# FFN weights turned by a transposing DMA on 16-bit planes instead of TensorE, with the background's turns redistributed

## The chip, the core and the metric

The kernel runs on one core of one Trainium2 chip, in one launch. The metric is device time in microseconds (us), the median of several executions. PE is TensorE, PEld its weight loads, DVE VectorE, ACT ScalarE, POOL GpSimd, and SP SyncE, which only issues DMAs here.

## The reference

One transformer block on x of shape (1, 2048, 1024), all in float32:

```python
x = x + attn(layernorm(x))        # q, k, v = xn @ w.T + b, seen as 32 heads of 32 channels
                                  # per token: softmax(q @ k.T / sqrt(32)) over the token's own 32 heads, then @ v
dq = lambda w: nf4_quant_dequant(w)   # per 64 values: absmax; nearest of 16 codes of w / absmax; code * absmax
h = silu(xn2 @ dq(w1).T) * (xn2 @ dq(w2).T)      # xn2 = layernorm(x); w1, w2: (2752, 1024)
x = x + h @ dq(w3).T                             # w3: (1024, 2752)
```

The scores are between the heads of one token, so they are many small 32 x 32 products. The quantising of w1, w2 and w3 is part of the computation and is done on the chip.

## The kernel before

**Three streams.** The foreground is first the attention, 16 tiles of 128 tokens, and then the FFN. In the background, from the first microseconds on, the FFN weights are quantised. A branch for inputs with other low bits (`fast=False`) is built too, and does not run here.

**Attention** (to about 569 us). For each tile i the loop from line 833 runs Q, K and V projections (`project`, L643: two halves of 16 matmuls each), the scores S and the weighted sums G (4 x 64 small matmuls in two parts), and `keep_T`, which transposes the normed tile and stores it to DRAM. Between them stand DVE's 32 x 32 transposes, its bias adds (L669, L685) and its softmax steps, and ACT's exponentials and norms.

**FFN.** There are 21 full chunks of 128 hidden rows, and one of 64. A `Unit` (L1406) does seven products of a Strassen-Winograd scheme for the gate and up projection of one chunk pair and 1024 tokens, eight matmul records each, into PSUM tiles z, q and rr. ACT copies z away between the products (L1424, L1431, L1438), and DVE multiplies gate and up (L1446, L1450). Behind the units of each of the first ten passes `down7` (L1509) does the down projection in seven products: ACT copies each result (L1532) and POOL issues accumulating DMAs into x1d in DRAM (L1534). There are 12 passes: six groups of chunks by two halves of the tokens; the last two end in the plain `down` (L1575). 41 units run after the plain first one; the page's L1446 x41 counts them.

**The background** is a Python generator, `background` (L283). It has 65 jobs: per chunk one for w1, one for w2 and one for w3, with a joint one for the half chunks of w1 and w2. Of these 63 have full blocks of 128 rows. A job takes a 128 x 1024 tile `wn` (3 buffers), scales it by its blocks' absolute maxima, makes eight band steps, and scales the result r (2 buffers) back. A band step is an ACT activation into an int8 tile (L299, 6 buffers) and a DVE add (L305; the first is L303). r goes to a second generator, `finish` (L205), which turns it in eight 128 x 128 blocks: four TensorE transposes into a PSUM tile `ptw` (L219), an ACT copy into the tile `wop` (L220), and both once more. When a pair is complete DVE makes the four sums and differences of the scheme (L226 to L229 and L232 to L235), and one DMA stores `wop` to DRAM (L238), from where `load_w12` (L455) and `load_w3` (L462) fetch it.

**What sets the order.** `advance(n)` (L357) adds n * 10/17 to an account, and takes one step of the generator for each whole turn. `spent(us)` does so in the FFN with us * RATE, after each product, and `flush` moves `finish` on. That gives an order in the program. The order on PE is the program's, since it is set by hand:

```python
    ctx.enter_context(tc.manual_schedule(engines={nc.tensor.engine}))
```

For ACT, DVE, POOL and SP a scheduler writes each engine's order at build time. It may draw an instruction forward past others when what it reads, and the buffer it writes, are free by its reckoning. On the chip each engine then works through its fixed order, and waits on semaphores. `hook["scale"]` tells who multiplies by the absolute maxima: ACT in the attention, DVE in `down7`, both in turn in the rest of the FFN.

Of the kernel before, what the change touches and what calls it, by code (L numbers as in the profile page):

```python
# [20 lines left out]
P = 128  # L21
# [11 lines left out]
HALF = F - NFULL * P  # L33
TB = 512
NTBP = S // (2 * TB)
RATE = 0.69
TURN = 10 / 17
XTAGS = ("B11", "B21", "B22", "T1", "T2", "T3", "T4")
XOPS = ("B11", "B12", "B21", "B22", "T1", "T2", "T3", "T4")
PAIRED = NFULL - 1  # L40
# [11 lines left out]
NNEG = 7  # L52
I8 = mybir.dt.int8
I32 = mybir.dt.int32
F32R = mybir.dt.float32r
LOW = 0xFFF

# [73 lines left out]
def forward(ctx, tc, const, fast, x, wqT, wkT, wvT, qb, kb, vb, w1, w2, w3, out):  # L131

    nc = tc.nc
    xf = x.flatten_outer_dims()
    of = out.flatten_outer_dims()
    ident, eps, mhalf = const["ident"], const["eps"], const["mhalf"]
# [15 lines left out]
    hook = {"scale": "ACT"}  # L152
# [49 lines left out]

    wops = {}

    def finish(kind, c, v):  # L205

        hn = min(P, F - c * P)
        q = hn if kind == "3" else P
        paired = kind == "3" and c < PAIRED
        second = kind == "2" or paired and c % 2  # L210
        if not second:
            wops["t"] = dqp.tile([P, 8, 4, P], FP, tag="wop", name="wop", bufs=1)
        o = wops["t"]
        first = 2 if second else 0
        for half in range(2):
            pt = hook["psum"](half)
            for k in range(4):
                j = 4 * half + k
                nc.tensor.transpose(pt[:q, k, :], v[:, j * q : (j + 1) * q], ident)  # L219
            nc.scalar.copy(o[:q, first + half], pt[:q])  # L220
            yield
        if kind == "1" or paired and not second:
            return
        if paired:
            b11, b12, b21, b22, t1, t2, t3, t4 = (o[:, n] for n in range(8))
            nc.vector.tensor_tensor(t1, b12, b11, ALU.subtract)  # L226
            nc.vector.tensor_tensor(t2, b22, t1, ALU.subtract)
            nc.vector.tensor_tensor(t3, b22, b12, ALU.subtract)
            nc.vector.tensor_tensor(t4, b21, t2, ALU.subtract)  # L229
        if kind == "2":  # L230
            a11, a12, a21, a22, s1, s2, s3, s4 = (o[:, n] for n in range(8))
            nc.vector.tensor_tensor(s1, a21, a22, ALU.add)  # L232
            nc.vector.tensor_tensor(s2, s1, a11, ALU.subtract)
            nc.vector.tensor_tensor(s3, a11, a21, ALU.subtract)
            nc.vector.tensor_tensor(s4, a12, s2, ALU.subtract)  # L235
        n = 8 if second else 2
        d = tc.dram_tile([q, n, 4, P], FP, name=f"wd{kind}_{c}")
        nc.sync.dma_start(d, o[:q, :n])  # L238
        wd[kind, c] = d
        if paired:  # L240
            wd[kind, c - 1] = d

    pending, step = [], {}
# [39 lines left out]
    def background():  # L283
        ready = load_w(*jobs[0])
        ahead = load_w(*jobs[1])
        am = absmax(*jobs[0], ready)
        yield
        for n, (kind, c) in enumerate(jobs):
            wn, wa = ready, am
            ready = ahead  # L290
            if n + 2 < len(jobs):
                ahead = load_w(*jobs[n + 2])
            w = width(kind, c)
            v = wn[:, :w]
            r = dqp.tile([P, E], FP, tag="r", name="r", bufs=2)[:, :w]
            for i, (lo, hi, scale, bias) in enumerate(BANDS):
                t = dqp.tile([P, E], I8, tag="sg", name="sg", bufs=6)[:, :w]
                with behind("step"):
                    nc.scalar.activation(t, v, AF.Copy, bias=bias, scale=scale)  # L299
                top = float(NF4_CODE[hi + 1])  # L300
                low = -1.0 if lo is None else float(NF4_CODE[lo])
                if i == 0:
                    nc.vector.tensor_scalar(r, t, top, low, ALU.min, ALU.max)  # L303
                else:
                    nc.vector._custom_dve(TENSOR_ADD_SAT, out=r, in0=r, in1=t, s0=top, s1=low)  # L305
                step["n"] = i
                yield
                if i == 4 and n + 1 < len(jobs):
                    am = absmax(*jobs[n + 1], ready)
                    yield  # L310
            engine = ("ACT", "DVE")[n % 2] if hook["scale"] == "both" else hook["scale"]
            scaled(r, r, wa, w // BLOCK, engine)
            pending.append(finish(kind, c, r))
            yield

    def low_bits():
# [40 lines left out]
    def advance(n):  # L357
        lent["turns"] += n * TURN
        while lent["turns"] >= 1:
            lent["turns"] -= 1  # L360
            with turn():
                next(bg, None)
# [99 lines left out]
    def load_w3(c):  # L462
# [10 lines left out]
            nc.sync.dma_start(t[r, :], src)  # L473
        return t

    def spent(us, finish=True):
        if finish and step["n"] in range(3, 8):
            flush(1)
        advance(us * RATE)

    def new_h():
        return hp.tile([P, TB], FP, tag="h", name="h", bufs=12)
# [48 lines left out]
    if fast:  # L531
# [111 lines left out]
        def project(m, i, n, take, first=lambda: None):  # L643

            ps = bank("pj")
            for k in range(KC):
                for part in xs[i]:
                    nc.tensor.matmul(  # L648
                        ps,
                        part[:, k, :],  # L650
                        W[m][k // 2][:, k % 2, ts(n, TB)],
                        start=k == 0 and part is xs[i][0],
                        stop=k == KC - 1 and part is xs[i][1],
                        skip_group_check=True,
                    )
            first()
            take(n, ps)
            advance(1)

        def qk(m, i, bias):  # L660
            tag = f"{m}d" if i != 1 else "xT1" if m == "q" else "xT0"
# [61 lines left out]
        def S(i, part):  # L723

            if not part:
                ats[i] = ps_at.tile([P, 4, 512], FP, tag="at", name="sc")
            at = ats[i]
            score(at, qd[i][0], kd[i][0], part)
            advance(1)
            if not part:  # L730
                return
            del qd[i], kd[i], ats[i]
            sc = at[:, :, 0:256].rearrange("p g (s t) -> p g s t", t=NH)
            mx = small.tile([P, 4, 8], FP, tag="mx", name="mx")
            nc.vector.tensor_reduce(mx, sc, AX.X, ALU.max)
            pr = work.tile([P, 32, NH], FP, tag="pr", name="pr")
            nc.vector.tensor_tensor(
                pr.rearrange("p (g s) t -> p g s t", g=4),
                sc,
                mx.unsqueeze(3).to_broadcast([P, 4, 8, NH]),  # L740
                ALU.subtract,
            )
            nc.scalar.activation(pr, pr, AF.Exp, scale=1.0 / math.sqrt(D))
            prT[i] = work.tile([P, 32, NH], FP, tag="prT", name="prT")
            nc.vector.transpose(prT[i], pr)

        def G(i, part):

            if not part:
                ats[i] = ps_at.tile([P, 4, 512], FP, tag="at", name="cx")  # L750
            at = ats[i]
            weigh(at, prT[i], part)
            advance(1)
            if not part:
                return
            del prT[i], ats[i]
            st = small.tile([P, 4], FP, tag="st1", name="st1", bufs=2)
            rs = small.tile([P, 4, 8], FP, tag="mx", name="rs")
            sums = at[:, :, : 8 * (D + 1)].rearrange("p b (s d) -> p b s d", d=D + 1)
            nc.vector.reciprocal(rs, sums[:, :, :, D])  # L760
            pr = work.tile([P, 32, NH], FP, tag="pr", name="pw")
            nc.vector.tensor_tensor(
                pr.rearrange("p (s b) d -> p b s d", b=4),
                sums[:, :, :, :D],
                rs.unsqueeze(3).to_broadcast([P, 4, 8, D]),
                ALU.mult,
            )
            x1 = xt.pop(i)
            cx = work.tile([P, E], FP, tag="cx", name="cx")
            nc.vector.transpose(  # L770
                cx.rearrange("p (h d) -> p d h", d=D), pr.rearrange("p s d -> p d s")
            )
            nc.vector.scalar_tensor_tensor(
                cx, x1, 1.0, cx, ALU.mult, ALU.add, accum_out=st[:, 0:1]
            )
            for n in range(2):
                nc.sync.dma_start(x1d[i][n], cx[:, ts(n, TB)])
            if i + 3 < NT:
                load_x(i + 3)
            hook["normed"] = norm(cx, cx, st, pr).ins  # L780
            x1n[i] = cx
# [51 lines left out]
        for i in range(2, NT):  # L833
# [28 lines left out]
            V(i, 1)  # L862
            flush(1)
            S(i, 0)
            advance(2)
        hook["scale"] = "both"
        left.close()

# [39 lines left out]
    else:  # L908
# [190 lines left out]
        with tc.issue_after(opening["first"]):  # L1099
            for n in range(2):  # L1100
                k = slice(2 * n, 2 * n + 2)
# [537 lines left out]
    for n, (g, tbp) in enumerate(passes):  # L1639
# [23 lines left out]
                hs[unit.c] = unit.last()  # L1663
        if sides:
            down7(g, tbp, sides)
        else:
            for _ in bg:
                pass
            down(g, tbp, hs)
# [41 lines left out]
```

## Time and profile before

| | |
|---|---|
| time, median of 3 runs (lowest, highest) | 2228.09 us (2227.78, 2230.97) |
| the profiled execution: its time, its span | 2224.73 us, 2222.9 us |
| busy of the span: PE, DVE, ACT, POOL | 96%, 63%, 59%, 12% |
| attention's tiles 2 to 16, from 67 to 569 us | DVE busy 417.28 us, PE 459.58 us, ACT 319.75 us |
| DMA, mean over the span | 181 GB/s |

The table's busy time is that of one profiled execution, from its first to its last instruction. A busy PE counts matmuls that overlap, so PE can read high where its matmuls are not dense. A group's row gives the line, engine, operation, tiles, and shapes; then the count, the busy time and the mean duration in ns, and last the idle time ahead of it with what ended it.

### The profile page before, as it was taken

To read this page: it belongs to the slowest core of one execution; us is meant where nothing else is said; L and a number is where in the kernel's file an instruction comes from. 1 tells how busy PE (TensorE), PEld (TensorE's weight loads), DVE (VectorE), ACT (ScalarE), POOL (GpSimd) and SP (SyncE) were. 2 spreads that over 40 slices of the span, in tenths; PEclk is the share of its full clock that TensorE was granted. 3 is DMA by queue.
4 is the path that set the end of the run, shared out by engine and by line. 5 is a ranking of instruction groups with operands and counts; after the bars stand their busy time and mean duration, and the time that the engine had idled before them with its cause. 6 is when DMAs were issued, how large, how long until landed. Compare 5 with 4: busy or idle time off the path is not lost.

```text
span 2222.9 us, 35192 instructions
## 1 busy us (share of the span) xinstructions
PE 2144.0 (96%) x14193; PEld 1148.3 (52%) x14193; DVE 1395.8 (63%) x1599; ACT 1302.8 (59%) x2635; POOL 275.4 (12%) x335
## 2 busy tenths in 40 slices
PE   7899989898999999999999999999999999999998
PEld 6677777776544444444444444444444444444432
DVE  6788877978666567565665756756656656453022
ACT  7667665756656657657657676586575676411200
POOL 1000000000003104013021030030120310401300
PEclk8899999999999999999999999999999999999999
DMA  8132323324669539579377694494983866965972
GB/s 294 40 126 68 116 68 107 119 85 160 239 240 263 140 123 250 191 266 196 125 196 190 247 243 133 148 224 165 320 181 123 182 173 256 259 208 141 259 286 96
DMA packets 154684, 402.73 MB, mean 181 GB/s; under 512 B 13648, under 2 KB 67920, under 8 KB 137360
## 3 DMA queue, kind: packets, MB, share of 16 engines
q1 hardware_dynamic: 113808, 326.92, 40.9%
q0 software_dynamic: 40704, 73.47, 19.6%
q8 instruction: 113, 1.85, 0.3%
q14 instruction: 59, 0.48, 0.1%
HBM read 227.07 MB, written 173.28 MB: 180 GB/s over the span
## 4 chain that ended last, share of the span: by engine, by line
PE 44%; issue 21%; DMA 5%; POOL 2%; DVE 1%; ACT 1%; POOLq 0%; SPq 0%; DVEq 0%; ACTq 0%
PE z L391 17%; PE q L391 8%; PE z L1519 7%; DMA x1d<-acc 4%; PE rr L391 4%; PE y L1519 4%; POOL x1d L1534 2%; PE r L1519 2%; PE po L1602 1%; PE ptw L219 1%; PE po L1613 1%; DMA wn<-in_wqT_dram 0%; DVE r L305 0%; ACT acc L1532 0%; DMA w<-wd 0%
## 5 line engine op out<-in xcount | busy, mean ns | idle before, releaser
L299 ACT ACTIVATE sg<-wn 128x1024 int8<-128x1024 f32 (+1 forms) x520 | 541.8, 1050 | 100.0 <-DVE r L305 87.8
L305 DVE CUSTOM_DVE_ANT_0 r<-r,sg 128x1024 f32<-128x1024 f32 (+1 forms) x455 | 552.0, 1213 | 22.2 <-ACT sg L299 1.6
L1534 POOL DMA_DIRECT2D x1d<-acc x280 | 243.9, 900 | 1247.0 <-ACT acc L1532 1196.8
L391 PE MATMUL z<-xB,w 128*128 128x512 f32 x720 | 323.4, 599 | 8.8 <-DMA w<-wd 4.9
L391 PE MATMUL z<-xT,w 128*128 128x512 f32 x656 | 294.9, 592 | 0.0
L391 PE MATMUL q<-xT,w 128*128 128x512 f32 x656 | 291.3, 592 | 0.0
L1519 PE MATMUL z<-w,h 128*128 128x512 f32 x496 | 231.2, 594 | 3.2 <-ACT acc L1532 3.0
L259 ACT ACTIVATE wn<-wn,rc 128x64 f32<-128x64 f32 x752 | 192.6, 336 | 62.6 <-DVE rc L279 59.1
L391 PEld LDWEIGHTS z<-xB,w 128*128 128x128 f32 x720 | 135.9, 192 | 170.8 <-issue 157.7
L391 PEld LDWEIGHTS q<-xT,w 128*128 128x128 f32 x656 | 123.3, 190 | 149.5 <-issue 147.6
L391 PEld LDWEIGHTS z<-xT,w 128*128 128x128 f32 x656 | 123.0, 190 | 146.8 <-issue 146.1
L1434 DVE TENSOR_TENSOR g<-g,rr 128x512 f32<-128x512 f32 x41 | 27.9, 681 | 210.3 <-PE rr L391 210.2
L220 ACT COPY wop<-ptw 128x512 f32<-128x512 f32 (+1 forms) x130 | 76.1, 586 | 134.8 <-PE ptw L219 122.8
L1519 PEld LDWEIGHTS z<-w,h 128*128 128x128 f32 x496 | 92.4, 190 | 115.4 <-issue 101.2
L303 DVE TENSOR_SCALAR r<-sg 128x1024 f32<-128x1024 int8 (+1 forms) x65 | 44.8, 689 | 169.2 <-PE ptw L219 152.8
L1519 PE MATMUL y<-w,h 128*128 128x512 f32 x320 | 148.8, 592 | 0.0
L391 PE MATMUL rr<-xB,w 128*128 128x512 f32 x328 | 147.5, 592 | 0.0
L1532 ACT COPY acc<-z 128x512 f32<-128x512 f32 x160 | 92.9, 581 | 84.8 <-PE z L1519 48.2
L259 ACT ACTIVATE r<-r,am 128x64 f32<-128x64 f32 x440 | 112.8, 341 | 5.2 <-DVE r L305 4.8
L648 PE MATMUL pj<-wk,xh 128*128 128x512 f32 x224 | 94.1, 420 | 14.8 <-DVE qd L667 14.6
L271 DVE TENSOR_REDUCE am<-wn 128x16 f32<-128x1024 f32 (+1 forms) x65 | 78.3, 1204 | 39.8 <-ACT r L259 37.1
L391 PEld LDWEIGHTS rr<-xB,w 128*128 128x128 f32 x328 | 61.5, 190 | 73.7 <-issue 73.7
(144 smaller groups left out, 2749.2 us busy)
## 6 DMA issues: line engine op xcount, KB each, us to landing
x1d<-acc POOLq DMA_DIRECT2D x280, 256.0 KB, 7.0
wd<-wop SPq DMA_DIRECT2D x31, 2048.0 KB, 9.0
w<-wd SPq DMA_DIRECT2D x41, 1280.0 KB, 7.0
wn<-in_w_dram SPq DMA_DIRECT2D x63, 512.0 KB, 6.1
xT<-xdT SPq DMA_DIRECT2D x28, 1024.0 KB, 7.1
xB<-xdB SPq DMA_DIRECT2D x24, 1024.0 KB, 7.3
w<-wd SPq DMA_DIRECT2D x44, 512.0 KB, 4.1
w<-wd SPq DMA_DIRECT2D x10, 1536.0 KB, 7.3
```

What stands on the lines that cost most here:

```text
L220: nc.scalar.copy(o[:q, first + half], pt[:q])
L259: nc.scalar.mul(dst[:, ts(n, BLOCK)], src[:, ts(n, BLOCK)], by[:, n : n + 1])
L271: nc.vector.tensor_reduce(am[:, :nb], v.rearrange("p (b e) -> p b e", e=BLOCK), AX.X, ALU.max, apply_absolute_value=True,)
L299: nc.scalar.activation(t, v, AF.Copy, bias=bias, scale=scale)
L303: nc.vector.tensor_scalar(r, t, top, low, ALU.min, ALU.max)
L305: nc.vector._custom_dve(TENSOR_ADD_SAT, out=r, in0=r, in1=t, s0=top, s1=low)
L391: nc.tensor.matmul(dst, w[:, k, :], xop[:, k, :], start=start and k == 0, stop=stop and k == 3, skip_group_check=True,)
L648: nc.tensor.matmul(ps, part[:, k, :], W[m][k // 2][:, k % 2, ts(n, TB)], start=k == 0 and part is xs[i][0], stop=k == KC - 1 and part is x ...
L1434: nc.vector.tensor_tensor(self.g0, self.g0, r, ALU.add)
L1519: nc.tensor.matmul(dst, side[n][:, ts(q, P)], w3T[g[2 * m]][:, W3[n]], start=start and m == 0, stop=stop and m == 1, skip_group_check=True,)
L1532: nc.scalar.copy(t, src)
L1534: nc.gpsimd.dma_start(x1d[8 * tbp + 2 * q + j][n], t, accum_op=ALU.add)
```

## The change

For the 63 full jobs `finish` no longer uses PE. ACT copies r, seen as 16-bit halves of the 32-bit words, into the job's own `wn` tile as two planes: all low halves, then all high halves (2048 elements a partition). SP issues one transposing DMA of 128 x 2048 16-bit elements from `wn` into a free part of `wop`. One instruction joins the planes to 32-bit words again, on POOL while `hook["scale"]` is "ACT", which is in the attention, and else on DVE. The two jobs of the half chunk keep the old way.

The turns are given differently. In the attention only the projections give some: 2 and 1 behind the two halves of K, 1 behind each half of V, none behind Q, S and G: 5 a tile, where it was 12 * 10/17 = 7.06. In the FFN the factor is 1.05 until the first `down7` has been issued and then 0.7, where it was 0.69 throughout.

```diff
-RATE = 0.69
+RATE = 0.7
+EARLY = 1.05
 TURN = 10 / 17
+TURNS = {("q", 0): 0, ("q", 1): 0, ("k", 0): 2, ("k", 1): 1, ("v", 0): 1, ("v", 1): 1}
...
-    def finish(kind, c, v):
+    def finish(kind, c, v, wn):
...
-        for half in range(2):
-            pt = hook["psum"](half)
-            for k in range(4):
-                j = 4 * half + k
-                nc.tensor.transpose(pt[:q, k, :], v[:, j * q : (j + 1) * q], ident)
-            nc.scalar.copy(o[:q, first + half], pt[:q])
+        if hn == P:
+            planes = wn.bitcast(U16).rearrange("p (two e) -> p two e", two=2)
+            turned = o[:, first + 4 : first + 6].rearrange("p n k d -> p (n k d)").bitcast(U16)
+            nc.scalar.copy(planes, v.bitcast(U16).rearrange("p (e two) -> p two e", two=2))
+            nc.sync.dma_start_transpose(
+                turned.rearrange("p (j h) -> p j h", h=P), wn.bitcast(U16)
+            )
             yield
+            joins = nc.gpsimd if hook["scale"] == "ACT" else nc.vector
+            joins.tensor_copy(
+                o[:, first : first + 2].rearrange("p n k d -> p (n k d)").bitcast(U16)
+                .rearrange("p (e two) -> p two e", two=2),
+                turned.rearrange("p (two e) -> p two e", two=2),
+            )
+            yield
+        else:
+            for half in range(2):
+                pt = hook["psum"](half)
+                for k in range(4):
+                    j = 4 * half + k
+                    nc.tensor.transpose(pt[:q, k, :], v[:, j * q : (j + 1) * q], ident)
+                nc.scalar.copy(o[:q, first + half], pt[:q])
+                yield
...
-            pending.append(finish(kind, c, r))
+            pending.append(finish(kind, c, r, wn))
...
+    pace = {"rate": EARLY}
+
     def spent(us, finish=True):
         if finish and step["n"] in range(3, 8):
             flush(1)
-        advance(us * RATE)
+        advance(us * pace["rate"])
...
@@ def project
-            advance(1)
+            advance(TURNS[m, n] / TURN)
@@ def S
-            advance(1)
@@ def G
-            advance(1)
@@ the loop over the tiles
-            advance(2)
@@ the loop over the passes
         if sides:
             down7(g, tbp, sides)
+            pace["rate"] = RATE
```

More of the change, by code (lines that the diff above doesn't have):

```diff
@@ L54 @@
 I32 = mybir.dt.int32
+U16 = mybir.dt.uint16
 F32R = mybir.dt.float32r
```

## The prediction

> **What bounds the kernel now.** I read the page's busy row first, then the busy times by stretch, then the groups that the change touches, and last who waited for whom.
>
> ```profile
> PE 2144.0 (96%) x14193; PEld 1148.3 (52%) x14193; DVE 1395.8 (63%) x1599; ACT 1302.8 (59%) x2635; POOL 275.4 (12%) x335
> ```
>
> ```profile
> 67.00:569.00 502.00, 459.58 (x9339) 369.65 (x9339) 417.28 (x447) 319.75 (x723) 20.51 (x28) 0.96 0.32 105
> 569.00:1357.00 788.00, 784.79 (x2380) 360.00 (x2381) 493.12 (x572) 519.40 (x1018) 122.43 (x141) 1.00 0.70 205
> 1357.00:2223.00 866.00, 846.61 (x2126) 376.93 (x2124) 437.33 (x524) 416.31 (x804) 122.04 (x140) 0.99 0.68 198
> ```
>
> The columns are PE, PEld, DVE, ACT, POOL, clock, DMA share, GB/s. The first stretch is attention's tiles 2 to 16, the second ends at the twentieth of 41 units. In the FFN PE has no idle time (784.79 of 788), with DVE at 63% and ACT at 66%. In the attention DVE is at 83% and PE's 92% holds waits: neither is full, each waits for the other.
>
> ```profile
> L305 DVE CUSTOM_DVE_ANT_0 r<-r,sg 128x1024 f32<-128x1024 f32 x448 | 547.1, 1221 | 21.3 <-ACT sg L299 1.6
> L219 PE MATMUL ptw<-ident,r 128*128 128x128 f32 x512 | 77.5, 274 | 3.8 <-DVE vd L680 2.0 <-ACT wop L220 1.8
> L220 ACT COPY wop<-ptw 128x512 f32<-128x512 f32 x128 | 75.0, 586 | 128.1 <-PE ptw L219 116.1 <-DMA wd<-wop 12.0
> L303 DVE TENSOR_SCALAR r<-sg 128x1024 f32<-128x1024 int8 x64 | 44.2, 691 | 160.1 <-PE ptw L219 152.8 <-ACT wn L259 7.3
> L255 DVE TENSOR_TENSOR r<-r,am 128x1024 f32<-128x1024 f32 x37 | 45.2, 1223 | 1.0
> L592 ACT ACTIVATE xn<-xt 128x1024 f32<-128x1024 f32 x14 | 14.7, 1047 | 1.4 <-DMA xt<-in_x_dram 1.4
> ```
>
> The 152.8 us are the point: a job's first DVE step waits until PE has turned an earlier r. PE's order is fixed by hand, so these transposes hold the background to its place in the program. A matmul's 274 ns contains its latency; the timeline has its price:
>
> ```profile
> 632.39 0.60 PE L219 MATMUL ptw<-ident,r 128*128 128x128 f32 x4
> ...
> 632.83 1.45 PE L391 MATMUL q<-xT,w 128*128 128x512 f32 x3
> ```
>
> Four transposes move the next product by 0.44 us.
>
> **Removed.** The two programs' orders show 520 transposes before and 16 after; 88 of the 504 lie in the attention, 416 in the FFN. 104 fours x 0.44 = 45.8 us, all on the bound engine: 25 us up to the twentieth unit, 21 us after. The attention's 88 (9.7 us) I credit nothing, since DVE will set its pace (below). 126 ACT copies go.
>
> **Added per job.** ACT's copy of 2048 halves: rows give 586 ns for 512 elements and 1047 for 1024, so 1.05 + 2 x 0.46 = 1.97 us against 2 x 0.586 removed. (Bounds: 1.05 if halves were as cheap as words, 2.1 as two L592.) The join of 2048: DVE's two-source rows, 1.223 us for 1024 and 0.685 for 512 (the scheme sums), give 0.147 fixed and 0.538 per 512. L303, one source, has 0.691 for 1024, so 0.544 behind the same fixed part, and 0.147 + 2 x 0.544 = 1.24 for 2048. At the two-source rate it is 2.3, at L303's own length 0.69; I take 1.24, as L303 is the nearest kind. 55 joins stand on DVE and 8 on POOL, where no row shows such a copy; POOL is busy 20.51 us of 502 there, so even 30 us each would fit, if it does not disturb DVE.
>
> The transposing DMA has no row. Nearest, by size and queue:
>
> ```profile
> wn<-in_w_dram SPq DMA_DIRECT2D x63, 512.0 KB, 6.1
> xdB<-xT SPq DMA_DIRECT2D x32, 256.0 KB, 2.9
> x1d<-acc POOLq DMA_DIRECT2D x280, 256.0 KB, 7.0
> ```
>
> So 2.9 to 14 us (the last row twice); I take 6.1. PE's waiting disappears from the background, and SP's grows: the load of a next `wn` now stands behind the transposing DMA that frees it, and the unit weights' loads (L458, L459), which PE waits for, behind both.
>
> The skill speaks for and against. "VectorE: DVE Perf Modes" (The three transpose paths) has 1309 ns for one 128 x 128 block by DMA and 390 by TensorE: 16 blocks one after another would be an estimated 20.9 us a job, 41 jobs 857 us, and the second stretch 64 us longer than the 793 I come to below. "DMA: Bandwidth & Descriptors" (Latency and other measured facts) has 261 GB/s for such transfers, an estimated 2.0 us. No trace here shows either.
>
> **Moved.** This decides. With no transposes on PE the scheduler draws the background far forward, though the program's turns in the attention become fewer. In DVE's order 84 adds stand ahead of the sixteenth tile's value bias before, 125 after. At the twentieth unit it is 294 against 414, and all 455 are done by the twenty-fourth, which before took until the thirty-sixth.
>
> Attention, 67 to 569 us, more work on DVE: 41 adds x 1.221 = 50.1; 7 scalings x 1.223 = 8.6; 12 scheme sums x 0.685 = 8.2; 8 joins x 1.24 = 9.9; 5 absolute maxima x 1.212 = 6.1; 5 first steps x 0.691 = 3.5; small ones 1.9. That is 88 us on 417: 505 us of DVE in a stretch of 502. DVE becomes the bound. It now idles for PE and for stores:
>
> ```profile
> DVE xU L527 <- DMA xdT<-xU: 23.6, 11, 4.1
> DVE kd L667 <- PE pj L648: 22.8, 9, 4.3
> ```
>
> The drawn-in work fills much of that, but not all, as the chain of softmax, PE and norm remains. Of 17% idle I take a third as left: 505/0.94 = 537, so +35 us (+4 if DVE never idled, +106 if it idled as now).
>
> FFN to the twentieth unit: on DVE 79 adds 96.5, 42 joins 52.1, 24 scheme sums 16.4, 11 scalings 13.5, 11 maxima 13.3, 13 first steps 9.0, small 4.6: +205, so 698 us. On ACT 95 steps x 1.056 (L299) = 100, 190 small multiplications x 0.256 (L259: 192.6 over 752) = 49, 40 copies x 1.97 = 79, less 58 x 0.586 = 34: +194, so 713 us. PE's own time falls to 788 - 25 = 763: DVE would be 91% busy, ACT 94%, where 63 and 66% left PE no wait. ACT's copies of z have the length of one product, 3.43 us, and a copy of 1.97 or a waiting step can now stand ahead. I take 4% of 763 as PE's loss, 30 us (0 to 6%).
>
> After that the background is gone, and PE alone counts: -21 us, and a stall at the end of the background goes:
>
> ```profile
> 1959.18 5.74 DMA wn<-in_wqT_dram
> ...
> 1966.27 5.20 DMA wn<-in_wqT_dram
> ...
> 1973.20 7.14 DMA w<-wd
> ```
>
> There the weights of a unit came late behind the low bits' loads (PE idle 5 us). After, these loads stand far ahead and apart: -5 us.
>
> Sum on the span: +35 - 25 + 30 - 21 - 5 = +14: 2222.9 + 14 = 2237. The profiled execution took 2224.73, the median is 3.4 us above that; on the median's scale 2228.1 + 14 = 2242. What a measurement of this kernel tells from no change is about 0.2%, 4.5 us.
>
> **Rivals.** *Faster*: the drawn-in work fits into idle time. The gain of 51 us (25 + 21 + 5) stands, and the losses are 19 us in the attention (DVE 97% busy) and 11 in the FFN (1.5%): 2207 us; with the least of both, 2181. It decides where the two losses together stay below 46 us. For it: a scheduler that draws forward only what fits; DVE's idle is mostly waits of 2 to 4 us, as long as two adds. Against: both engines above 90%, in fixed orders, leaning on each other.
>
> *Much slower*: the transposing DMA lands late. Where DVE does the scaling, the joins that stand too close behind it in DVE's order (4.4 us of work in the closest case) lack about 17 us in all if ACT's copy and a landing of 6.1 are waited for, and some 177 us at 14 us. DVE's idle in that stretch, 763 - 698 = 65 us, covers landings to about 9 us; at 14 us 112 us more: about 2350.
>
> *No change*: losses of 46 to 55 us. The background would be done earlier and nothing won.
>
> **How the numbers follow.** Forecast (moderately slower, 2234 to 2280) 0.43; faster 0.34; much slower 0.11; within 0.2% 0.12. So faster 0.34, same 0.12, slower 0.54. The range reaches down past the faster case's middle, to 2194, and up to 2325, into the late landing; a tenth is left out on each side.
>
> **What would show it.** Right: attention's end (the first `z` of L391 after the last scores) moves from 569 to about 604 us, DVE above 92% busy there; adds end at about the twenty-fourth unit; then DVE below 25% and PE without gaps; `ptw` 16 in all. PE gaps in the first half of the FFN would be put to ACT's copies of z or to a late `w`. Wrong: attention's end below 585, or PE at 100% in the first FFN half (then the faster case); joins waiting for the DMA over 50 us in all (then the slower); or a transposing DMA that keeps SP busy for more than a job's 19 us.

## The result and the profile after

| | before | after |
|---|---|---|
| time, median of 4 runs (lowest, highest) | 2227.94 us (2226.94, 2230.97) | 2367.63 us (2355.33, 2377.67) |
| the profiled execution: time, span | 2224.73 us, 2222.9 us | 2355.33 us, 2353.4 us |
| mean granted clock | 0.983 | 0.957 |

The changed kernel is slower, by a ratio of 1.0608 (95% interval 1.058 to 1.0635). The forecast was 2242 us with a range of 2194 to 2325: the direction is right, the size far off. Of its cases, the one that comes nearest is the "much slower" rival at 2350 us, which had 0.11.

The stretches were cut at the same events as in the prediction: the sixteenth tile's value bias (569 us before, 588 after) and the twentieth unit (1357 before, 1504 after). The busy row of the page comes first, then the busy times by stretch with the columns of before (PE, PEld, DVE, ACT, POOL, clock, DMA share, GB/s):

```profile
PE 2126.1 (90%) x13689; PEld 1104.4 (47%) x13689; DVE 1434.7 (61%) x1655; ACT 1328.5 (56%) x2556; POOL 303.1 (13%) x343
```

```profile
67.00:588.00 521.00, 457.15 (x9146) 364.02 (x9147) 492.19 (x532) 384.69 (x797) 42.18 (x35) 0.94 0.45 133
588.00:1504.00 916.00, 790.76 (x2151) 340.88 (x2151) 670.66 (x776) 682.27 (x1293) 126.73 (x142) 0.94 0.88 221
1504.00:2320.00 816.00, 799.20 (x1873) 349.40 (x1871) 211.53 (x273) 212.45 (x375) 120.94 (x140) 0.99 0.66 175
```

The middle row is the result. The stretch grew from 788 to 916 us, and PE, which had next to no idle time there, is idle for 125 of the 916, at a clock of 0.94. DVE and ACT are not full: 73% and 74%. What grew is the last but one column, the DMA share, from 0.70 to 0.88. The groups and the waits of the whole span name what stands there (a wait's row: who waited for what, us in all, times, longest):

```profile
L227 DVE COPY wop<-wop 128x2048 uint16<-128x2048 uint16 x55 | 72.8, 1324 | 164.1 <-DMA wop<-wn 164.0
L221 ACT COPY wn<-r 128x2048 uint16<-128x2048 uint16 x63 | 119.4, 1895 | 20.2 <-DVE r L274 11.5
```

```profile
DVE wop L227 <- DMA wop<-wn: 164.0, 30, 25.0
...
PE z L1537 <- ACT acc L1550: 91.3, 15, 23.7
...
ACT acc L1550 <- DMA x1d<-acc: 27.0, 12, 8.7
```

The joins take what was priced (1.324 us each, against 1.24), and the copies too (1.895 against 1.97). What was not priced is ahead of the joins: 164 us of waiting for the transposing DMA. Its landing, worked out from each issue in the trace, has a median of 5.2 us over the 56 with a recorded end, less than the 6.1 that the prediction took, and a mean of 8.3. For the 17 that are in flight together with accumulating stores of `down7` the median is 12.9 and the longest 30.7; the other 39 have 4.7 and at most 8.0. One such place in the timeline (start, length, engine, line, operation; in brackets the idle time before it and what ended it):

```profile
1058.71 33.58 SPq L222 DMA_TRANSPOSE wop<-wn  x2
...
1082.14 1.88 PE L1537 MATMUL y<-w,h 128*128 128x512 f32 x4
1089.43 1.31 DVE L227 COPY wop<-wop 128x2048 uint16<-128x2048 uint16 x1 [25.00 <-DMA wop<-wn]
1092.39 7.93 SPq L203 DMA_DIRECT2D wn<-in_w_dram  x2
1099.99 1.31 DVE L227 COPY wop<-wop 128x2048 uint16<-128x2048 uint16 x1 [9.25 <-DMA wop<-wn]
...
1106.37 0.82 ACT L278 ACTIVATE wn<-wn,rc 128x64 f32<-128x64 f32 x3 [25.61 <-DVE rc L297]
...
1107.71 1.22 PE L1537 MATMUL z<-w,h 128*128 128x512 f32 x1 [23.69 <-ACT acc L1550]
```

Read it as a chain. SyncE is held for 33.6 us in issuing two transposing DMAs (18.4 and 15.1). DVE stands in the join for 25 us, then 9 us more. ACT has a scaling in its fixed order that needs DVE's next result, and stands for 25.6 us. Behind that scaling stand ACT's copies of the down projection's results, and PE, which needs their PSUM tiles, stands for 23.7 us. Five gaps of 9 to 24 us in this half's down projections sum to 82 of the 125 us. PE's busy time, which was to fall from 784.79 to 763 us, is 790.76, at the lower clock.

### The profile page after: what moved, and what is told of

The parts are those of the page before. It is cut to its first block, busy times and chain, and to the rows that moved or that the text cites. A ratio compares the mean times of both kernels' runs of the same rounds, so it can differ in the third digit from the quotient of the medians.

```text
span 2353.4 us, 34247 instructions
## 1 busy us (share of the span) xinstructions
PE 2126.1 (90%) x13689; PEld 1104.4 (47%) x13689; DVE 1434.7 (61%) x1655; ACT 1328.5 (56%) x2556; POOL 303.1 (13%) x343
## 3 DMA queue, kind: packets, MB, share of 16 engines
q1 hardware_dynamic: 244848, 359.96, 49.4%
q0 software_dynamic: 40704, 73.47, 19.7%
## 4 chain that ended last, share of the span: by engine, by line
PE 31%; issue 21%; DMA 11%; ACT 6%; DVE 4%; POOL 1%; DVEq 0%; SPq 0%; POOLq 0%; ACTq 0%
PE z L410 11%; PE z L1537 6%; DMA wop<-wn 5%; PE q L410 5%; DMA x1d<-acc 4%; PE y L1537 3%; ACT sg L318 3%; PE rr L410 2%; DVE r L324 2%; PE r L1537 2%; ACT wn L278 1%; PE po L1620 1%; ACT wn L221 1%; DMA wn<-in_w_dram 1%; PE po L1631 1%
## 5 line engine op out<-in xcount | busy, mean ns | idle before, releaser
L318 ACT ACTIVATE sg<-wn 128x1024 int8<-128x1024 f32 (+1 forms) x520 | 520.9, 1047 | 87.5 <-DVE r L324 35.5
L410 PE MATMUL z<-xT,w 128*128 128x512 f32 x656 | 301.8, 603 | 22.4 <-ACT u L1449 12.9
L1537 PE MATMUL z<-w,h 128*128 128x512 f32 x496 | 238.3, 610 | 57.2 <-ACT acc L1550 57.0
L227 DVE COPY wop<-wop 128x2048 uint16<-128x2048 uint16 x55 | 72.8, 1324 | 164.1 <-DMA wop<-wn 164.0
L221 ACT COPY wn<-r 128x2048 uint16<-128x2048 uint16 x63 | 119.4, 1895 | 20.2 <-DVE r L274 11.5
L1449 ACT COPY u<-z 128x512 f32<-128x512 f32 x41 | 23.7, 578 | 179.1 <-PE z L410 179.1
L669 PE MATMUL pj<-wk,xh 128*128 128x512 f32 x224 | 96.1, 429 | 14.6 <-DVE qd L688 14.0
L669 PE MATMUL pj<-wq,xl 128*128 128x512 f32 x224 | 94.9, 424 | 9.2 <-DVE xl L642 9.2
```

The source lines that it names most:

```text
L221: nc.scalar.copy(planes, v.bitcast(U16).rearrange("p (e two) -> p two e", two=2))
L227: joins.tensor_copy(o[:, first : first + 2].rearrange("p n k d -> p (n k d)").bitcast(U16) .rearrange("p (e two) -> p two e", two=2), turn ...
L410: nc.tensor.matmul(dst, w[:, k, :], xop[:, k, :], start=start and k == 0, stop=stop and k == 3, skip_group_check=True,)
L669: nc.tensor.matmul(ps, part[:, k, :], W[m][k // 2][:, k % 2, ts(n, TB)], start=k == 0 and part is xs[i][0], stop=k == KC - 1 and part is x ...
L1449: nc.scalar.copy(u2, self.z)
L1537: nc.tensor.matmul(dst, side[n][:, ts(q, P)], w3T[g[2 * m]][:, W3[n]], start=start and m == 0, stop=stop and m == 1, skip_group_check=True,)
```

## The experiments

**Theories.** LANDING: the transposing DMA lands late beside the stores, and that costs the time. LOAD: the drawn-in band work fills DVE and ACT, and PE waits for those. CLASH is LANDING made narrow: the transposing DMA and the accumulating stores delay each other on the DMA engines. Each run is given with its ratio to runs of the kernel before on the same chip; "by the first unit" and the like are shifts of that event against before, in the profiled executions.

**1. Only the new turns** (the kernel before, with TensorE's transposes and the changed `TURNS`, `RATE` and `EARLY`).

> The change's turns (2, 1 behind K, 1, 1 behind V, 1.05 in the first FFN pass, then 0.7) with the TensorE transposes kept. Two theories for the 140 us that the changed kernel is slower. LANDING: transposing DMAs that are issued while down7's accumulating DMAs and the operand loads fill the DMA queues land 20 to 30 us later, DVE stands in order at the join, ACT behind DVE, PE behind ACT. LOAD: the background drawn far forward fills DVE and ACT above 90% and PE loses to that whatever the DMA does. Neither puts the loss into the turns: in the built order 63 adds stand ahead of the sixteenth tile's value bias (84 before, 125 changed), so attention is some 10 to 25 us shorter than before and the FFN as before: 2200 to 2230 us. Over 2250 would say that the turns themselves cost.

Measured: 2228.9 us, 0.9961 (0.9939 to 0.9983). The turns by themselves cost nothing; they even gain some 0.4%.

**2. Only the transposing DMA** (after, with the old turns: `RATE = EARLY = 0.69`, `advance(1)` behind the products as before).

> The transposing DMA with the old turns (10/17 of a turn behind each piece of attention, 0.69 throughout the FFN). The built order draws the background forward almost as in the changed kernel (125 adds at the sixteenth tile, 413 at the twentieth unit, all by the twenty-fourth), so both theories expect what the changed kernel has: 2340 to 2395 us. Under 2300 would say that the new turns, not the DMA path, cost most.

Measured: 2392.11 us, 1.0683 (1.0642 to 1.0723). So all of the loss comes with the new way of turning.

**3. No transposing DMA.** The join reads the planes, so the weights are not turned.

```diff
-            nc.sync.dma_start_transpose(
-                turned.rearrange("p (j h) -> p j h", h=P), wn.bitcast(U16)
-            )
...
-                turned.rearrange("p (two e) -> p two e", two=2),
+                planes,
```

> The changed kernel with the transposing DMA left out: the join reads the planes where ACT put them, so the FFN weights are not turned and the output is another. All else stays, with the background drawn forward as far (123 adds at the sixteenth tile, 406 at the twentieth unit). LANDING: the joins no longer wait, the FFN's PE gaps of 10 to 24 us go, and 90 us or more of the 130 come back: 2180 to 2270 us, with attention still 10 to 25 us longer than before. LOAD: DVE and ACT are as full as ever, so at least two thirds of the loss stays: 2310 us or more.

Measured: 2258.94 us, 1.0108 (1.0081 to 1.0135). Joins, copies and drawn-in adds are all there, and five percentage points of six are gone (0.050 x 2228 = 111 us). The busy times by stretch, cut at the same events:

```profile
68.00:600.00 532.00, 466.58 (x9278) 370.67 (x9279) 489.78 (x528) 384.60 (x789) 53.80 (x35) 0.93 0.35 114
600.00:1412.00 812.00, 772.57 (x2045) 336.42 (x2032) 657.75 (x766) 667.52 (x1262) 126.98 (x142) 0.98 0.75 220
```

The FFN stretch is 812 us at nearly the same DVE and ACT work as the 916 of after. LOAD is left with what this kernel still loses: 31 us by the end of the attention, 48 by the first unit, 34 at the end. (The attention's end is placed to some 15 us only: run 7, whose program is that of after up to there, has it 34 us later than before, and after 20.)

**4. The load taken away instead.** After, but from the FFN on each band step is queued in ACT's order behind ACT's latest product copy. In DVE's order 58 adds then stand ahead of the sixteenth value bias (125 in after) and 287 by the twentieth unit (414).

```diff
+        urgent["rule"] = ("step",)
...
-            nc.scalar.copy(self.g0, self.z)
+            marked(nc.scalar.copy(self.g0, self.z))
```

> The changed kernel with ACT's band steps queued behind the latest copy of a product by ACT from the FFN's start on, so that the scheduler can't draw the background forward: 58 adds at the sixteenth tile, 287 at the twentieth unit, 455 at the thirty-sixth, much as before the change. DVE and ACT fall to some 65 to 72% busy in the FFN. LOAD: the loss goes and PE's 46 us are won: 2175 to 2225 us. LANDING: transposing DMAs still fall into down7 and land late, in ten passes instead of six; DVE and ACT have slack to catch up but ACT's copies still stand behind: 2230 to 2330 us.

Measured: 2316.9 us, 1.0385 (1.0342 to 1.0428). The attention ends 21 us earlier than before, where after ended 20 later: that part is LOAD's, and it is more than the scatter. But from the first unit to the end it loses 102 us (from -17 to +85), with the load where it used to be: joins wait 191.0 us for the DMA.

**5. Paced, and no transposing DMA** (edits 3 and 4 together).

> The kernel with paced band steps (2316.9), and without the transposing DMA: the join reads the planes, so the weights are not turned. LANDING: what is left of the loss there is the DMA's, and TensorE's 504 transposes are gone with the background in its old place: the gain of 46 us shows, 2175 to 2215. LOAD or JOINS (the joins on VectorE and the copies on ScalarE hold up the products wherever they stand): above 2240.

Measured: 2181.4 us, 0.9755 (0.9712 to 0.9798). Without the DMA the gain of removing TensorE's transposes shows. The FFN to the twentieth unit, and PE's waits for the copies in `down7` over the whole span (91.3 us in after):

```profile
560.00:1343.00 783.00, 763.00 (x2149) 337.94 (x2148) 560.16 (x641) 577.16 (x1079) 125.58 (x141) 0.99 0.72 210
```

```profile
PE z L1535 <- ACT acc L1548: 8.3, 7, 1.6
```

PE is busy for 763.00 us, the figure that the prediction worked out as 788 - 25. The stretch itself is only 5 us shorter than before, as PE is now idle for 20 us of it, 9.3 of them in one wait for a down projection's weights.

**6. A plain DMA of the same bytes in the same place** (rows of 4 KB, so nothing is turned).

```diff
-            nc.sync.dma_start_transpose(
-                turned.rearrange("p (j h) -> p j h", h=P), wn.bitcast(U16)
-            )
+            nc.sync.dma_start(turned, wn.bitcast(U16))
```

> The changed kernel with the transposing DMA made a plain one: the same 512 KB go from the planes to the same place, in rows of 4 KB, so the weights are not turned. LANDING BY FORM (the transposing DMA is late because it is split into 256-byte packets, some 2,048 of them): the plain transfer lands in 3 to 6 us beside the accumulating stores as well, the join's waits for it fall below 60 us in all, and the time is near that of the kernel without any DMA there (2259): 2250 to 2285. LANDING BY PLACE (any transfer of 512 KB that is issued beside the accumulating stores is late): landings there stay above 10 us, and the time is 2330 to 2375.

Measured: 2285.25 us, 1.0219 (1.0175 to 1.0262), just above what LANDING BY FORM expected (2250 to 2285). The DMA lands in a median of 3.3 us, DVE's joins wait 46.5 us. But beside the accumulating stores it too is late: a median of 7.3 us and at most 18.5 over 17, where 3 to 6 was expected, against 3.0 elsewhere. So place counts as well as form. Some two thirds of the whole loss (6.08% against 2.19%) go with the form: SyncE's queue carries 244,848 packets in after, and 122,880 here, and an issue holds SyncE for 0.5 us in the median, where it was 3.0. Which of the two costs was not separated.

**7. The accumulating stores made plain** (after, without `accum_op=ALU.add`; the sums over the passes are not formed).

> The changed kernel with the accumulating stores of the down projection made plain stores of the same size from the same place, so the sums over the passes are not formed. CLASH (the transposing DMA is late because the accumulating stores, which read and write DRAM, fill the DMA engines beside it): landings beside them fall from a median of 12.9 us to 5 to 7, and the time to 2255 to 2300. OWN (the transposing DMA is late by itself, or through the loads of weights): landings and time stay, 2335 to 2370.

Measured: 2276.35 us, 1.0174 (1.0131 to 1.0216). Landings beside the stores fall from a median of 12.9 to 7.8 us (5 to 7 was expected). Either partner of the clash, taken away, brings back most of it.

**8. The same two edits on the paced kernel** (4 and 7 together). All transposing DMAs and all waits for them are there.

> The kernel with paced band steps and all its transposing DMAs and waits, with the accumulating stores made plain ones, so the sums over the passes are not formed. CLASH between the two kinds of DMA: the loss against the paced kernel without a transposing DMA (2181) falls from 136 to under 70 us: 2190 to 2250. If the transposing DMA is late by itself: 2290 or more.

Measured: 2178.39 us, 0.9756 (0.9721 to 0.979): as fast as with no transposing DMA at all. This run and run 4 differ in one argument of one call. From the DMA part of both pages, first the paced kernel, then this one (queue: packets, MB, share of 16 engines' span; then a store's landing):

```profile
q0 software_dynamic: 40704, 73.47, 19.6%
...
x1d<-acc POOLq DMA_DIRECT2D x280, 256.0 KB, 8.6
```

```profile
q0 software_dynamic: 22784, 73.47, 9.0%
...
x1d<-acc POOLq DMA_DIRECT2D x280, 256.0 KB, 4.2
```

And their waits, in the same order:

```profile
DVE wop L227 <- DMA wop<-wn: 191.0, 36, 25.9
...
ACT acc L1551 <- DMA x1d<-acc: 107.3, 56, 8.5
```

```profile
DVE wop L227 <- DMA wop<-wn: 70.1, 36, 7.8
...
ACT acc L1551 <- DMA x1d<-acc: 9.3, 9, 2.0
```

The accumulating stores take more than twice the engines' time for the same bytes, and with the transposing DMA both sides land late. Plain stores without a transposing DMA were not run; but in run 5, with accumulating stores, PE waits only those 8.3 us in all for `down7`'s copies, so plain stores could give little by themselves. CLASH holds. That the two meet on the DMA engines fits the DMA share (in the second down projection 1.07 in the paced kernel and 0.80 here); no run tells the engines from the memory or the ports behind them.

**9 to 13. By which way does a late DMA cost time?** Each run takes one wait away and keeps the transfers. In all of them the sums are written over their operands and the store takes that half twice, except in run 10, which leaves nothing out.

*9, no join waits*: the DMA stays, the join reads the planes.

> The changed kernel with every transposing DMA in its place and of its size, but nobody on VectorE waits for it: the join reads the untransposed planes, the four sums are written over their operands, and the store takes that half twice, so the weights are wrong. The next load of the tile, on SyncE, still waits for the transposing DMA. WAIT (VectorE stands in the join until the late DMA has landed, behind it ScalarE's steps and product copies, and so TensorE): near the kernel without the DMA (2259): 2250 to 2290. CONTENTION (the 256-byte packets and SyncE's long issues delay the loads of unit weights and the other stores whoever waits for the join): 2325 to 2370.

Measured: 2347.37 us, 1.0502 (1.0467 to 1.0536). This lies in CONTENTION's range, and WAIT as stated is refuted. The wait has a new place, since the next load stands behind the transposing DMA on SyncE:

```profile
DVE am L298 <- DMA wn<-in_w_dram: 118.9, 15, 27.5
```

*10, the join later* (paced; one more `yield` ahead of the join, and the join pinned behind the latest band add in DVE's order).

> The kernel with paced band steps (2316.9), with the join in the FFN one call of the finishing generator later, and pinned in VectorE's order behind the latest band add. Nothing is left out. WAIT: the joins' waits for the DMA fall from 191 us to under 90, and the time to 2230 to 2290. CONTENTION: the waits fall as well, but the time stays at 2300 to 2320, since the loads and stores are late.

Measured: 2299.42 us, 1.0251 (1.0211 to 1.0292), within 1 us of what CONTENTION expected. Joins wait 80.3 us in place of 191.0, as both expected, and ACT waits 120.7 us for accumulating stores. More slack for the join alone is worth little.

*11, the DMA reads r* (as 9, but its source is `v`, so the load's tile comes free earlier).

> As the kernel in which nobody waits for the transposing DMA in a join (2347), and it reads r itself, not the planes, so that the next load's tile is free when the join has read it. The transposing DMAs have their number, size and places; the weights are wrong. RELEASE (the loads of wn are late because their tile is held until the late DMA has landed): the waits of the absolute maximum for wn fall from 119 us to under 50, 2260 to 2300. QUEUE (they are late because SyncE itself is held up in issuing the transposing DMA, and the loads stand behind it in its queue) or CONTENTION (the engines are full): 2320 to 2360, and the waits for wn stay above 80 us.

Measured: 2342.84 us, 1.0494 (1.0451 to 1.0537). The wait for `wn` fell to 28.3 us, so most of it had been the tile's release; the time did not follow, for now the first band step waits for r, and ACT for stores:

```profile
ACT acc L1558 <- DMA x1d<-acc: 66.8, 26, 10.3
DVE r L330 <- DMA wop<-r: 53.2, 7, 17.4
```

*12, the loads of `wn` on GpSimd's queue* (11, with `nc.gpsimd.dma_start` in `load_w`).

> The kernel above with the loads of wn issued by GpSimd in place of SyncE: they no longer stand behind the transposing DMA in a queue, and the bytes on the DMA engines are the same. QUEUE: 2260 to 2300, waits for wn under 50 us. CONTENTION: 2320 or more, since loads and accumulating stores are slow whoever issues them; ScalarE's waits for accumulating stores above 60 us (27 in the changed kernel).

Measured: 2369.79 us, 1.0613 (1.0584 to 1.0643). QUEUE is not borne out by the time. CONTENTION's time came, its other sign did not: ACT waits 42.7 us for accumulating stores, where over 60 was expected. And the run is a poor test, since its attention ended 59 us later than before's (run 11: 23), and the wait for r stayed (72.6 us).

*13, paced, and the DMA reads a resident operand tile in the FFN*, so that no band work waits for it.

> The kernel with paced band steps, with all transposing DMAs of the same size in the same places, but in the FFN they read a resident operand tile and not the job's own; the join reads the planes and the sums are written over their operands, so the weights are wrong. Nothing of the band work waits for a transposing DMA now: not the join, not the load's tile, not r. VectorE's order has the same counts as in the paced kernel with the DMA (2316.9) and without it (2181.4). WAITS (the whole cost is engines that stand for a late transposing DMA, now in one place, now in another): 2185 to 2230. CONTENTION (it slows the other transfers): 2270 to 2320, with ScalarE waiting over 100 us for accumulating stores.

Measured: 2378.98 us, 1.0652 (1.058 to 1.0723), above everything expected. The transposing DMAs beside the stores land later still (median 25.8 us), SyncE's queue holds the loads, and ACT waits for stores:

```profile
ACT acc L1562 <- DMA x1d<-acc: 194.2, 64, 15.5
DVE am L301 <- DMA wn<-in_w_dram: 131.7, 10, 31.4
```

So the clash is paid wherever somebody first needs one of the delayed transfers: the join, the next load, r, or the store buffers. How much each way costs by itself stays open, since no run had only one of them.

**14. TensorE turns what is finished within a down projection** (20 of the 63 jobs), the transposing DMA the others (43 are in its trace: 8 in the attention, 35 in the FFN).

```diff
-        if hn == P:
+        if hn == P and hook["scale"] != "DVE":
```

> The changed kernel, but a job that is finished within the down projection of a pass is turned by TensorE as before (4 transposes, a copy, twice); elsewhere by the transposing DMA. Some 20 of the 63 jobs go back. LANDING: no transposing DMA is issued beside the accumulating stores, all landings are below 9 us, and the scheduler draws less forward (98 adds by the sixteenth tile, 298 by the twentieth unit): the loss of the first half of the FFN goes, 2225 to 2260. LOAD (the drawn-in work is what costs): in the FFN the same, since the work is drawn in less here; so this run alone doesn't part them, and stands for a version to use. If it is above 2300 both are wrong.

Measured: 2248.33 us, 1.0049 (1.003 to 1.0069).

**15. Both repairs** (4 and 14), **16. the same once more, and 17. pacing with TensorE alone** (run 1 and edit 4).

> Both repairs: paced band steps, and within the down projections TensorE turns the blocks (28 jobs), elsewhere the transposing DMA (35 jobs). From the kernel paced without the DMA (2181) plus 28 jobs x 0.88 us of TensorE (25 us), plus some 10 us of waits for landings of 4.7 us: 2200 to 2230, a ratio of 0.985 to 0.998. If the transposing DMA costs as much elsewhere as within the down projections (CONTENTION in another form), 2240 to 2270.

Measured: 2217.98 us, 0.9923 (0.9901 to 0.9946).

> The kernel with both repairs once more, on the chip of the run without the transposing DMA: 2210 to 2225 again, a ratio of 0.988 to 0.996.

Measured: 2214.81 us, 0.993 (0.9909 to 0.9951).

> No transposing DMA at all: the kernel before with the new turns and with paced band steps, TensorE turning all 63 jobs. It tells whether the gain of the kernel with both repairs (2218) is the pacing's or the transposing DMA's. If the DMA's: 35 jobs x 0.88 us = 31 us of TensorE more, less what its waits cost, so 2225 to 2240. If the pacing's: 2210 to 2222.

Measured: 2227.31 us, 0.999 (0.9975 to 1.0006), beside run 16. The expectation of run 15 counts 28 jobs for TensorE and 35 for the DMA; the 35 are those in the FFN, and the traces of runs 15 and 16 have 20 and 43. Pacing with TensorE alone gains nothing that can be measured, so the gain, 0.6% of run 16 against run 17, is the transposing DMA's, used where the DMA engines have room. (Against the new turns alone, run 1, the distance is some 0.3%, and the intervals overlap a little.) From the kernel of run 15, the FFN to the twentieth unit and the joins' waits:

```profile
545.00:1348.00 803.00, 775.77 (x2237) 347.72 (x2236) 547.33 (x629) 569.88 (x1089) 123.69 (x141) 0.99 0.78 219
```

```profile
DVE wop L227 <- DMA wop<-wn: 29.4, 18, 7.4
```

The kernel of runs 15 and 16 is 0.7% faster than before, and faster than after by more than 6%.

## Why the prediction was right or wrong, point by point

**The landing: the step that failed.** The prediction took 6.1 us for every transposing DMA, from the loads of `wn`, counted on 65 us of DVE's idle time to cover them, and gave the case of 14 us a chance of 0.11. Against the median landing of 5.2 us 6.1 was not even low. What was wrong was the use of one number for all places: beside the accumulating stores the landing was 12.9 us in the median and up to 30.7, the 65 us did not cover that, and DVE waited 164.0 us in the joins. With the transposing DMA taken out the kernel took 2258.94 us (run 3), near the 2242 that the sum gave, so this term holds most of the miss. By the program's order 20 of the 63 jobs are finished within down projections (run 14), and there the DMA engines were full before the change. A stretch of the kernel before shows it, the first down projection, which the prediction does not use:

```profile
684.00:737.00 53.00, 52.04 (x136) 23.59 (x135) 36.88 (x41) 39.60 (x68) 23.98 (x27) 1.00 1.07 271
```

The DMA share is 1.07 (records of packets can overlap), where the prediction's stretch had a mean of 0.70. The row that it priced from held the warning as well: of the 47 loads of `wn` before with a recorded end, 16 fell beside accumulating stores, with a median of 7.7 us and up to 12.3, and 31 elsewhere, with 4.0. The late rival's arithmetic was right in kind: waits beyond DVE's idle time turn into time of PE. At 2350 us it came within 18 us, but that is partly luck: it took 14 us for all joins, where the trace has 4.7 in the median for most and 5 to 31 for the 17 beside the stores, and it had no lower clock in it.

**Attention, +35 taken.** After, +20 at the sixteenth value bias; in the kernel without the DMA, +31; the scatter of this event is some 15 us. DVE was to be busy for 505 us at 94%; it was busy for 492.19 of 521, which is 94%. The mechanism and, within the scatter, its size hold. Run 4 shows it from the other side: 67 adds fewer there, and the end moves from +20 to -21.

**TensorE's transposes, -25 and -21, and the stall, -5.** Right as work removed, and seen only where the clash is gone: 763.00 us of PE in run 5, and from the twentieth unit to the end 2181.7 - 1343 = 839 us, where before had 866. Of the first part's 25 us run 5 keeps only 5 as time, since PE is idle there for 20. In after itself the last part gained 16 us of the 26. A gap of 8.2 us at 2079 us is in it, behind DVE's work on the low bits after the last job's late join (its DMA landed in 14.6 us); but the kernel without the DMA has a gap of 5.7 at the like place, so little of it is shown to be the landing's.

**PE's loss from fuller DVE and ACT, +30.** About right, from the kernel without the DMA. The work itself was put somewhat high (DVE 698 us and ACT 713, in after 670.66 and 682.27; and 713 of 763 is 93%, not 94). From its first unit (680 us) to the twentieth (1412) it takes 732 us, where before took 726 with the transposes. As the nineteen units between hold most of the 25 us removed, some 29 us were lost to load. Not foreseen were some 17 us between the attention's end and the first unit (80 us against 62), in the short part where both streams meet.

**What would show it.** Joins waiting over 50 us in all was the sign for the slower case: 164. The adds were done by the twenty-fourth unit, and 16 `ptw` were left, as said. PE without gaps after that was wrong, by the gap at 2079 us. SyncE busy for more than 19 us was named as a danger: single issues reach 18.4 us, and two in a row held it for 33.6.

**The rules that were weighed.** A transposing DMA of sixteen blocks landed in 4.2 us at best and 5.2 in the median. From the Trainium skill's "VectorE: DVE Perf Modes" (The three transpose paths), block after block, the estimate was 20.9 us, and from its "DMA: Bandwidth & Descriptors" (Latency and other measured facts) 2.0: the measurement lies between, and decides. What bears on the result is another section of the second page, "Issuing engines are not separate DMA queues": DMAs started from different engines end on the same 16 DMA engines and interleave. The traces are in line with it: GpSimd's stores land in a median of 8.6 us in the paced kernel, which has SyncE's transposing DMAs, and in 7.3 in run 5 without them.

## What to carry to other kernels

Price a new transfer from the stretch in which it will land, and look at the DMA share there, not at its mean: where the share was near 1, as in the down projections, the added transfers landed late, the plain copy too (7.3 us against 3.0), and with the transposing ones the stores that were there before as well (8.6 us against 7.3). Look next at who stands behind each late transfer in an engine's fixed order, for when one wait is taken away the next one takes its place (join, load, r, store buffers). Moving work from a full engine to the DMA paid where the DMA had room: in the paced kernel, turning 43 jobs by DMA and 20 by TensorE gained 0.7%, and turning all 63 by DMA lost 3.85% (6.1% unpaced).

## What the runs showed of the hardware that was not expected

- Issuing a transposing DMA of 512 KB from SBUF to SBUF keeps SyncE itself busy: 1.3 us at least, 3.0 in the median, and 18.4 at most, at a place where the DMA share was 1.1 (1058 to 1108 us). The next DMAs of that queue stand behind it: the loads of `wn` at 1092.39 us follow two such issues, of 33.6 us together.
- It is split into packets of 256 bytes: SyncE's queue grew from 113,808 packets to 244,848, for 33 MB more, and the packets under 512 bytes from 13,648 to 144,688.
- An accumulating store to DRAM takes more than twice the DMA engines' time of a plain one (19.6% of the span against 9.0% for the same 73.47 MB), and 40,704 packets in place of 22,784.
- The granted clock was lower where PE had gaps: 0.94 in the stretch that lost most, 0.98 without the transposing DMA, 0.99 when paced as well. What it adds to the loss was not separated by a run; PE's busy time there is 790.76 us at 0.94 and 763.00 at 0.99, for as many matmul records (2151 and 2149), so 28 us is an estimate.
- A copy of 2048 16-bit elements a partition, with a stride of two on one side, takes 1.324 us on DVE, 1.895 on ACT and 2.602 on GpSimd.
